# P1 and P2 of the second product on two levels in blocks k=1 and k=2 of an fp32 AdaLN and expert FFN kernel

## Chip, core and metric

The kernel runs on one core of a Trainium2 chip, in fp32. The metric is the device time of one execution in microseconds (us). Five engines work side by side, each through its own queue in order: TensorE (PE; its weight loads are listed as PEld), VectorE (DVE), ScalarE (ACT), GpSimd (POOL) and SyncE (SP), which issues the transfers. They wait for each other by semaphores.

## What is computed

The reference, cut to what matters (B, N, D = 64, 64, 512; six experts of rank 16, the two largest gates are kept):

```python
def cond(v, q, W3, b3, W2, b2):
    q_emb = relu(q @ W3 + b3)
    v_sum = sum(v, axis=1, keepdims=True)
    x = (n * v + v_sum) * q_emb[:, None, :]
    return relu(x @ W2 + b2)

def ffn(x, W_base, b_base, A_s, B_s, A_r, B_r, W_router, b_router):
    base_out = x @ W_base + b_base
    shared_out = (x @ A_s) @ B_s
    gates = softmax(x @ W_router + b_router)
    # w_per_e: the gates of the two largest experts, 0 for the others
    hw = einsum('bsd,edr->bser', x, A_r) * w_per_e[..., None]
    routed_out = einsum('bser,erf->bsf', hw, B_r)
    return base_out + shared_out + routed_out

out = x + ffn(cond(x, cond_1024, ...), ...)
```

There are two wide products of 4096 rows by 512 by 512: the first with `W2` (it makes `y`), the second with `W_base`. The narrow product multiplies `y` by 118 columns: shared and expert factors, and the router's logits.

## The kernel before

The 4096 rows are four blocks of 1024, k = 0 to 3 ("blocks 1 to 4" in the change's title words, so blocks 2 and 3 are k=1 and k=2). Features lie on the 128 partitions, rows along the free axis. Each wide product is done by Strassen's scheme in Winograd's form: its operands are quartered and seven products P1 to P7 of half size take the place of eight. `row_sums` (L261) forms the sums of the row side, `weight_sums` (L133) those of the weights. A product of half size is, for each of two output chunks j, `product` (L174): two matmuls of 128x512. An fp32 matmul appears in the trace as two records.

The scheme can be applied again inside a product ("two levels"): a half-size product then becomes seven inner products of 128x256, which the code calls `q(n, t)`: n = 1 to 7 is the inner product, t the outer product in the order in which they run. The text calls them Q1 to Q7. They share two PSUM banks per outer product, a and b, each of two halves of 256 columns. Q1 and Q2 go to a's low half, Q5 and Q3 to its high half, Q6 to b's low half (on top of a copy of Q1, `seed_y`), Q7 and Q4 to b's high half (on top of a copy of Q1+Q6, `seed_z`). What has to be read in between leaves by `take_w5` (Q5), `take_u` (Q1+Q6), `take_22` (after Q7), `take_1` (after Q2 and Q3) and `take_21` (after Q4). Where the outer product has something to be added to (`plus`), a take is a DVE addition; where it has nothing (`plus` is None), ACT copies the part.

The first product is on two levels in k = 1, 2, 3 (`first_inner`, L431). The second product is on one level in k = 0, 1, 2 (`second`, L658), and partly on two in k = 3 (`second_inner`, L759), where Q1, Q5, Q6 of P1 stand among the narrow products (`two[6]`, `two[7]` in the loop at L1058).

In `second` PSUM banks are called x (P1, then P2 on top), y (a copy of P1, then P6), z (a copy of y, then P7 and P4) and w (P5, then P3), each for j = 0 and 1. ACT makes the copies (`seed`, L670). `with_x` (L676) adds the input rows, which have been loaded to `res` (L648), by DVE. `gate` (L607) makes softmax and top 2 on DVE with one Exp on ACT, `weigh` (L584) multiplies on DVE, `turn` (L593) transposes on TensorE into `hwT`, `difference` (L602) makes `hwd` on POOL, and `routed` (L682) adds the expert part to the banks.

The next block's preparation is spread over all this by hand: `prepare` (L284) fills a list `behind`, and `fill` (L279) takes items from it at fixed places; `share` (L698) does so in `second`. An item is a pair of batches (ACT, L218: one batch of 64 rows of one chunk is multiplied by q and N and gets its sum added, in place in `x`), or a pair of reductions with their multiplication (DVE, L213 and L214), or a row sum. `nq` (L212) is N times q. The order of the instructions on each engine is that of the code.

Six PSUM banks ("pp") rotate among the banks of the products; SBUF tiles with one tag share one place.

Of the kernel before, what the change touches and what calls it, by code (L numbers as in the profile page):

```python
# [1 line left out]

# [7 lines left out]
F32 = mybir.dt.float32  # L10
# [5 lines left out]
P = 128  # L16
# [21 lines left out]
def adaln_ffn(ctx: ExitStack, tc: tile.TileContext, xa, x0, x1, head, w3, w2, wb, a, bcat, bb, br, outT):  # L38
# [108 lines left out]
    def inner_weight_sums(w, t, it, pairs=(5, 6, 7, 4), engine=nc.vector):  # L147


        order = (*pairs, 1, 2, 3)  # L150
        at = {i: n for n, i in enumerate(order)}
        step = 3 // (len(pairs) - 1)

        def side(o, n):
            b = {1: t[o][:, 0, :P], 2: t[o][:, 1, :P], 3: t[o][:, 1, P:]}
            return b[n] if n in b else it[:, {5: 0, 6: 1, 7: 2, 4: 3}[n], at[o]]

        low = w.rearrange("p (o k) m -> p o k m", k=KH)
        n = len(pairs)
        groups = ((slice(0, n), lambda c, m: t["sums"][:, ::step, c, ts(m, P)]),  # L160
                  (slice(n, n + 2), lambda c, m: low[:, :, c, ts(m, P)]),
                  (slice(n + 2, n + 3), lambda c, m: t[3][:, c, ts(m, P)].unsqueeze(1)))
        steps = []
        for o, b in groups:
            i = [it[:, n, o] for n in range(4)]
            steps += [
                lambda i=i, b=b: engine.tensor_tensor(i[0], b(0, 1), b(0, 0), ALU.subtract),
                lambda i=i, b=b: engine.tensor_tensor(i[1], b(1, 1), i[0], ALU.subtract),
                lambda i=i, b=b: engine.tensor_tensor(i[2], b(1, 1), b(0, 1), ALU.subtract),
                lambda i=i, b=b: engine.tensor_tensor(i[3], b(1, 0), i[1], ALU.subtract),  # L170
            ]
        return side, steps
# [26 lines left out]
    def modulate(k):  # L199
# [6 lines left out]
        def sums(c, half):  # L206

            bs = ts(half, BB // 2)
            xc = v[:, c].rearrange("p h (b n) -> p b h n", n=NH)[:, bs]
            q = q_sb[:, c, ts(k, BB)]  # L210
            if half == 0:
                nc.vector.tensor_scalar(nq[:, c], q, float(N), None, ALU.mult)  # L212
            nc.vector.tensor_reduce(vsum[:, c, bs], xc, AX.XY, ALU.add)  # L213
            nc.vector.tensor_tensor(vsum[:, c, bs], vsum[:, c, bs], q[:, bs], ALU.mult)  # L214
# [69 lines left out]
    def prepare(k, also=()):  # L284
# [6 lines left out]
        ss[k], row_steps = row_sums(vs[k], "s")  # L291
        early, late = row_steps(slice(0, 1)), row_steps(slice(1, 2))
# [56 lines left out]
    def first_mixed(y):  # L349
# [30 lines left out]
        p1 = mid.tile([P, KH, cols], F32, tag="p1", name="p1_0")  # L380
# [277 lines left out]
    def second(k, y, ph, res):  # L658
# [44 lines left out]
        gate(k, ph)  # L703
        prod(1, 0, "x")
        seed("y", "x", 0)
        prod(1, 1, "x")
        seed("y", "x", 1)
        prod(6, 0, "y", start=False)
        seed("z", "y", 0)
        prod(2, 0, "x", start=False)  # L710
        weigh(k, ph)
        u12, u22 = {}, {}
        u12[0] = with_x("y", 0, KH, 0)
        share()
        prod(7, 0, "z", start=False)
        u22[0] = with_x("z", 0, KH, 1)
        prod(6, 1, "y", start=False)
        seed("z", "y", 1)
        u12[1] = with_x("y", 1, KH + 1, 0)
        share()  # L720
        prod(2, 1, "x", start=False)
        prod(7, 1, "z", start=False)
        u22[1] = with_x("z", 1, KH + 1, 1)
        hwT = turn(k)
# [33 lines left out]

    def second_inner(k, y, res):  # L759
# [3 lines left out]
        t_side = wide["t"]  # L763
# [5 lines left out]
        x11, x12, x21, x22 = res[0, 0], res[1, 0], res[0, 1], res[1, 1]  # L769
        plus = {1: None, 2: x11, 5: None, 4: x21, 3: x12}  # L770
        out = {1: p1, 2: x11, 5: p5, 4: x21, 3: x12}

        place = {1: (0, (0, 1, 2, 3)), 2: (1, (0, 1, 2, 3)), 5: (1, (3, 1, 2, 0)), 4: (2, (0, 1, 2, 3)),
                 3: (3, (0, 1, 2, 3))}
        sy = {}
        add = lambda o, a, b, engine=nc.vector: engine.tensor_tensor(o, a, b, ALU.add)

        def sums_of(o, a, engine=nc.vector):
            i, at = place[o]
            return inner_row_steps(lambda n: plain[:, at[n], i], a, engine)  # L780
# [7 lines left out]

        def s_side(o, n):
            a = sy[o]  # L790
            direct = {1: a[:, 0, lo], 2: a[:, 1, lo], 4: a[:, 1, hi]}
            if n in direct:
                return direct[n]
            i, at = place[o]
            return plain[:, at[{5: 0, 6: 1, 7: 2, 3: 3}[n]], i]
# [17 lines left out]
        bank, hws = {}, {}  # L813

        def open_banks(t):
            for n in "ab":
                bank[n, t] = ps_p.tile([P, TB], F32, tag="pp", name=f"j{n}_{k}_{t}")

        def accumulate(p, w, s, start=False):
            nc.tensor.matmul(p, w, s, start=start, stop=True, skip_group_check=True)  # L820

        def q(n, t):
            o = order[t]
            b, cols = {1: ("a", lo), 2: ("a", lo), 5: ("a", hi), 3: ("a", hi), 6: ("b", lo), 7: ("b", hi), 4: ("b", hi)}[n]
            accumulate(bank[b, t][:, cols], t_side(o, n), s_side(o, n), n == 1)

# [16 lines left out]

        def seed_y(t):
            nc.scalar.copy(bank["b", t][:, lo], bank["a", t][:, lo])

        def seed_z(t):
            nc.scalar.copy(bank["b", t][:, hi], bank["b", t][:, lo])

        def take(t, src, at, j, cols):  # L850

            c, e = out[order[t]][:, j, cols], plus[order[t]]
            if e is None:
                nc.scalar.copy(c, src[:, at])
            else:
                add(c, src[:, at], e[:, j, cols])

        def passed_on(t, j, cols):
            o = order[t]
            if o == 5:  # L860
                add(x12[:, j, cols], x12[:, j, cols], p5[:, j, cols])
                add(x22[:, j, cols], x22[:, j, cols], p5[:, j, cols], nc.gpsimd)
            if o in (5, 4, 3):
                f, h, t = {5: (KH, 1, x22), 4: (0, 1, x21), 3: (KH, 0, x12)}[o]
                j = slice(j, j + 1) if isinstance(j, int) else j
                queue = nc.scalar if o == 3 and cols == hi else nc.sync
                queue.dma_start(
                    outT[k, f + j.start : f + j.stop, h, :, cols].rearrange("f p t -> p f t"), t[:, j, cols]
                )

        take_w5 = lambda t: take(t, bank["a", t], hi, 1, hi)
        take_u = lambda t: take(t, bank["b", t], lo, 1, lo)

        def take_22(t):
            r = out[order[t]][:, 1, hi]
            add(r, bank["b", t][:, hi], r)
            passed_on(t, 1, hi)

        def take_1(t):
            a, c, e = bank["a", t], out[order[t]], plus[order[t]]  # L880
            if e is c:
                add(c[:, :, lo], a.rearrange("p (j t) -> p j t", j=KH), c[:, :, lo])
            else:
                take(t, a, lo, 0, lo)
                add(c[:, 1, lo], a[:, hi], c[:, 1, lo])
            passed_on(t, slice(0, KH), lo)

        def take_21(t):
            take(t, bank["b", t], hi, 0, hi)
            passed_on(t, 0, hi)  # L890
# [21 lines left out]
        def main_part(ph):  # L912
# [5 lines left out]
            def first():  # L918
                q(7, 0)
                q(3, 0)  # L920
                q(6, 1)
                seed_z(1)
                q(2, 0)
                take(0, bank["a", 0], lo, 0, lo)
                take_w5(1)
                take_22(0)

            gate(k, ph, (first, lambda: add(p1[:, 1, lo], bank["a", 0][:, hi], p1[:, 1, lo])))
# [90 lines left out]
    inner_t, inner_steps = inner_weight_sums(  # L1019
        w2_sb, t2, const.tile([P, 4, 7, P], F32, tag="inner_t", name="inner_t")  # L1020
    )


    wide = {}
# [3 lines left out]
        0: [lambda: nc.gpsimd.tensor_tensor(bcat_d, bcat_pairs[:, :, 0], bcat_pairs[:, :, 1], ALU.subtract)]  # L1028
    }

    def wide_sums():
        place = xpool.tile([P, NC, 2, TB], F32, tag="x", name="inner_tb").rearrange("p c h t -> p (c h t)")
        wide["t"], steps = inner_weight_sums(
            wb_sb, tb, place[:, : 20 * P].rearrange("p (n o m) -> p n o m", n=4, o=5), (5, 4), nc.gpsimd
        )
        beside[1], beside[2] = steps[:4], steps[4:]

    for k in range(NB):
# [18 lines left out]
        two = second_inner(k, y, res) if k == NB - 1 else None  # L1057
        for n, (h, s) in enumerate(groups):  # L1058
            if rest and n == 2:
                rest()  # L1060
                if two:
                    two["sums"]()
            if two and n in two:
                two[n]()
# [5 lines left out]
        if two:  # L1070
# [5 lines left out]
        fill(4 if k else 9)  # L1076
        second(k, y, ph, res)
# [51 lines left out]
```

## Time and profile before

| | |
|---|---|
| median of 3 runs | 259.87 us (259.43 to 259.95) |
| profiled execution | 259.86 us, its span 258.1 us |
| mean granted TensorE clock | 0.997 |
| narrow product to the end of the second product, k=1 | 94.44 to 134.59 us of the span: 40.15 |
| the same, k=2 | 155.98 to 196.13: 40.15 |
| TensorE busy in each of these two stretches | 39.99 of 40.15 |
| HBM traffic | 110 GB/s over the span |

A line of the timeline has the start and length in us, engine, line of the code, operation, output and inputs with shapes, how many instructions were merged, and in brackets the engine's idle time before it with what ended it. The length of a merged PE line is not its spacing, since ends overlap: spacing is read from the starts of the following lines. A line of the page's first part has the busy time, share of the span and number of instructions of each engine. The chain line is the span split by what the last instruction was waiting for, step by step backwards.

### The profile page before, as it was taken

Reading aid. Unit: us, or ns where it says so; the run is one execution under the profiler, and the core shown is the slowest. Engines: PE = TensorE matmul, PEld = TensorE weight load, DVE = VectorE, ACT = ScalarE, POOL = GpSimd, SP = SyncE. Lnnn points to the kernel's source line nnn. Section 1 sums busy time; section 2 is a strip of 40 time slices with the busy share of each in tenths; the row PEclk is TensorE's granted clock in tenths of the full one; section 3 lists DMA queues with packets and bytes.
Section 4 is the critical chain, followed back from the end, with each engine's and each line's share of the span. In section 5 each row is a group of like instructions: output and inputs, shape, how many; then the busy total and the mean of one; then the engine's idle time right before and its main releaser. Section 6 shows DMA issues by size and latency. Waiting matters only on the chain.

```text
span 258.1 us, 3326 instructions
## 1 busy us (share of the span) xinstructions
PE 252.6 (98%) x1034; PEld 170.6 (66%) x1034; DVE 199.6 (77%) x404; ACT 142.7 (55%) x391; POOL 68.8 (27%) x88
## 2 busy tenths in 40 slices
PE   7999999999999999999999999999999999999994
PEld 3755896454468889445448888744446889975783
DVE  2899898789958976967995894996896476887473
ACT  2399587597037897279106889439603527443220
POOL 1000000012008520005104650000920864039950
PEclk9999999999999999999999999999999999999998
DMA  6998729403320035000431023300232003600054
GB/s 174 369 341 297 290 79 379 192 3 122 122 81 0 4 143 183 0 3 0 163 123 41 0 83 118 130 0 3 104 140 81 0 6 128 193 1 3 0 183 142
DMA packets 14675, 28.54 MB, mean 111 GB/s; under 512 B 1489, under 2 KB 3537, under 8 KB 14658
## 3 DMA queue, kind: packets, MB, share of 16 engines
q1 hardware_dynamic: 14370, 28.08, 30.9%
q10 hardware_dynamic: 288, 0.26, 0.3%
q8 instruction: 8, 0.13, 0.2%
q14 instruction: 9, 0.07, 0.1%
HBM read 19.94 MB, written 8.39 MB: 110 GB/s over the span
## 4 chain that ended last, share of the span: by engine, by line
PE 94%; ACT 2%; DMA 2%; SPq 0%; issue 0%; DVE 0%
PE ia L453 13%; PE ph L1066 11%; PE ib L453 10%; PE oz L176 9%; PE ox L176 8%; PE ow L176 8%; PE py L361 5%; PE oy L176 5%; PE ja L820 4%; PE ow L683 4%; PE jb L820 4%; PE ox L683 2%; PE oz L683 2%; DMA w_sb<-in_w_dram 2%; PE yw L176 1%; PE pt L597 1%
## 5 line engine op out<-in xcount | busy, mean ns | idle before, releaser
L218 ACT ACTIVATE x<-x,vsum,nq 128x64 f32<-128x64 f32 x192 | 67.5, 431 | 6.8 <-DVE vsum L214 6.8
L604 POOL TENSOR_TENSOR hwd<-hwT 113x512 f32<-113x512 f32 x4 | 5.6, 1393 | 109.4 <-ACT hwT L599 109.4
L1066 PEld LDWEIGHTS ph<-a_sb,y 128*128 128x128 f32 x256 | 30.3, 192 | 1.3 <-ACT y L347 0.7
L1066 PE MATMUL ph<-a_sb,y 128*128 128x118 f32 x256 | 30.8, 276 | 0.3 <-ACT y L347 0.3
L459 ACT COPY ib<-ia 128x256 f32<-128x256 f32 x21 | 7.6, 361 | 42.3 <-PE ia L453 42.3
L444 DVE TENSOR_TENSOR u<-ib,u 128x256 f32<-128x256 f32 x42 | 16.4, 418 | 18.6 <-PE ib L453 18.5
L176 PE MATMUL ox<-y,wb_sb 128*128 128x512 f32 x48 | 22.1, 593 | 0.0
L444 DVE TENSOR_TENSOR u<-ia,u 128x256 f32<-128x256 f32 (+1 forms) x36 | 16.1, 461 | 2.9 <-ACT u L491 1.6
L347 ACT ACTIVATE y<-u,head_sb 128x256 f32<-128x256 f32 (+1 forms) x30 | 15.8, 584 | 3.8 <-DVE u L419 3.1
L453 PE MATMUL ib<-inner_s,inner_t 128*128 128x256 f32 x60 | 17.8, 384 | 0.0
L213 DVE TENSOR_REDUCE vsum<-x 128x8 f32<-128x512 f32 x24 | 16.2, 675 | 0.0
L176 PEld LDWEIGHTS ox<-y,wb_sb 128*128 128x128 f32 x48 | 8.9, 190 | 10.0 <-issue 9.6
L176 PE MATMUL oz<-sy,tb 128*128 128x512 f32 x32 | 15.2, 599 | 0.0
L361 PE MATMUL py<-v,w_sb 128*128 128x512 f32 (+1 forms) x40 | 14.4, 510 | 0.8 <-DMA w_sb<-in_w_dram 0.8
L176 PE MATMUL oy<-sy,tb 128*128 128x512 f32 x32 | 14.9, 594 | 0.0
L307 POOL TENSOR_TENSOR inner_two<-x 128x256 f32<-128x256 f32 x3 | 2.2, 727 | 45.0 <-PE ib L453 45.0
L462 ACT COPY ib<-ib 128x256 f32<-128x256 f32 x21 | 7.6, 363 | 9.9 <-PE ib L453 9.9
L453 PEld LDWEIGHTS ib<-inner_s,inner_t 128*128 128x128 f32 x60 | 11.2, 190 | 2.2 <-ACT ib L462 0.8
L256 ACT ACTIVATE v<-x,vsum,nq 128x64 f32<-128x64 f32 x32 | 11.0, 430 | 1.9 <-DVE vsum L254 1.9
L361 PEld LDWEIGHTS py<-v,w_sb 128*128 128x128 f32 x40 | 7.4, 190 | 6.5 <-issue 4.5
L176 PE MATMUL oz<-y,tb 128*128 128x512 f32 x24 | 11.3, 592 | 0.0
L176 PE MATMUL ow<-sy,tb 128*128 128x512 f32 x24 | 11.3, 592 | 0.0
(236 smaller groups left out, 545.0 us busy)
## 6 DMA issues: line engine op xcount, KB each, us to landing
xu<-in_x_dram SPq DMA_DIRECT2D x16, 512.0 KB, 3.7
out_dram<-xu SPq DMA_DIRECT2D x29, 256.0 KB, 2.0
x<-in_x_dram SPq DMA_DIRECT2D x12, 512.0 KB, 7.6
x<-in_x_dram SPq DMA_DIRECT2D x7, 256.0 KB, 5.6
w_sb<-in_w_dram SPq DMA_DIRECT2D x4, 256.0 KB, 5.6
wb_sb<-in_wb_dram SPq DMA_DIRECT2D x4, 256.0 KB, 4.8
out_dram<-xu SPq DMA_DIRECT2D x4, 128.0 KB, 1.7
w_sb<-in_w_dram SPq DMA_DIRECT2D x1, 384.0 KB, 5.2
```

Source lines behind the costliest of these rows:

```text
L176: nc.tensor.matmul(ps, w[i][:, c, ts(j, P)], s[i][:, c, :], start=start and c == 0, stop=c == KH - 1, skip_group_check=True,)
L213: nc.vector.tensor_reduce(vsum[:, c, bs], xc, AX.XY, ALU.add)
L218: nc.scalar.activation(x, x, AF.Identity, bias=vsum[:, c, b : b + 1], scale=nq[:, c, b : b + 1])
L256: nc.scalar.activation(v[:, c, :, ts(b, NH)], batches_of(c, b, b + 1)[:, :, 0], AF.Identity, bias=vsum[:, c, b : b + 1], scale=nq[:, c, b ...
L347: nc.scalar.activation(y[:, f, h, cols], src, AF.Relu, bias=b2_sb[:, f : f + 1])
L361: nc.tensor.matmul(p[:, :, lo * NH : hi * NH], w2_sb[:, c, ts(f, P)], v[:, c, :, lo * NH : hi * NH], start=(c == 0 and lo == 0), stop=(c = ...
L444: add = lambda o, a, b: nc.vector.tensor_tensor(o, a, b, ALU.add)
L453: nc.tensor.matmul(bank[b, t][:, cols], t_side(o, n), s_side(o, n), start=n == 1, stop=True, skip_group_check=True,)
L459: nc.scalar.copy(bank["b", t][:, lo], bank["a", t][:, lo])
L683: nc.tensor.matmul(ps[name, j], bcat_sb[:, ts(f, P)], hw, start=False, stop=True, skip_group_check=True)
L820: nc.tensor.matmul(p, w, s, start=start, stop=True, skip_group_check=True)
L1066: nc.tensor.matmul(ph[:, h * NS + s, :HC], y[:, c, h, ts(s, P)], a_sb[:, c, :], start=(c == 0), stop=(c == NC - 1),)
```

## The change

P1 and P2 of the second product go on two levels in k=1 and k=2. The helpers of `second_inner` move to `inner_tools`, so that both use them, and the row side's places to `row_places`; the new `two_products` holds P1 and P2. P1's Q1, Q5 and Q6 stand among the last two narrow products. `second` gets a second branch for these blocks: banks y and x no longer accumulate P1 and P2 from products on one level, but get P1 by an ACT copy from SBUF; P2 is added to the loaded rows by POOL. The transposes come between the two products of P7. `fill(4)` moves from behind the row sums to the place ahead of P1's Q1.

P1 and P2 lie in a tile with the tag `s`, which the next block's row sums also use; so `prepare` now takes that tile at the first row sum, no longer at its own start. The weight sums of P1 and P2 (`low_t`) are formed once, by POOL in k=0, and k=3 uses them too. `p1_0` of k=0 moves to another tag. N times q is formed for all chunks in one instruction.

```diff
@@ modulate
-            if half == 0:
-                nc.vector.tensor_scalar(nq[:, c], q, float(N), None, ALU.mult)
+            if half == 0 and c == CHUNKS[0]:
+                nc.vector.tensor_scalar(nq, q_sb[:, :, ts(k, BB)], float(N), None, ALU.mult)
@@ prepare
-        ss[k], row_steps = row_sums(vs[k], "s")
-        early, late = row_steps(slice(0, 1)), row_steps(slice(1, 2))
+        made = []
+
+        def row_step(c, n):
+            if not made:
+                ss[k], row_steps = row_sums(vs[k], "s")
+                made.extend(row_steps(slice(c, c + 1)) for c in range(KH))
+            made[c][n]()
+
+        early, late = ([lambda c=c, n=n: row_step(c, n) for n in range(4)] for c in range(KH))
...
+    def two_products(k, y, res):
+
+        parts = mid.tile([P, 4, KH, TB], F32, tag="s", name=f"parts_{k}")
+        plain = mid.tile([P, 4, 4, R2], F32, tag="inner_s", name=f"inner_y_{k}")
+        p1, p2 = parts[:, 0], parts[:, 1]
+        operand = {1: y[:, :KH, 0], 2: y[:, KH:, 0]}
+        s_side, sums_of = row_places(plain, lambda o: operand[o], {o: (o - 1, (0, 1, 2, 3)) for o in (1, 2)})
+        tools = inner_tools(k, "h", (1, 2), low_side, s_side, {1: None, 2: None}, {1: p1, 2: p2})
+        for o in (1, 2):
+            for step in sums_of(o, lambda c, r, o=o: operand[o][:, c, ts(r, R2)], nc.gpsimd):
+                step()
+
+        def first_part():
+            tools.open_banks(0)
+            tools.q(1, 0)
+            tools.q(5, 0)
+            tools.seed_y(0)
+            tools.take_w5(0)
+
+        def second_part():
+            tools.q(6, 0)
+            tools.seed_z(0)
+            tools.take_u(0)
+
+        def third_part(ph):
+
+            tools.open_banks(1)
+            tools.q(1, 1)
+            tools.q(5, 1)
+            tools.seed_y(1)
+
+            def first():
+                tools.q(7, 0)
+                tools.q(3, 0)
+                tools.q(6, 1)
+                tools.seed_z(1)
+                tools.q(2, 0)
+                tools.take_11(0)
+                tools.take_w5(1)
+                tools.take_u(1)
+                tools.take_22(0)
+
+            gate(k, ph, (first, lambda: tools.take_12(0)))
+            tools.q(4, 0)
+            tools.take_21(0)
+            tools.q(7, 1)
+            tools.take_22(1)
+            tools.q(3, 1)
+            tools.q(2, 1)
+
+        def fourth_part():
+            tools.q(4, 1)
+            tools.take_21(1)
+            tools.add(res[0, 0], res[0, 0], p2, nc.gpsimd)
+
+        return {6: first_part, 7: second_part, "gate": third_part, "end": fourth_part, "p1": p1,
+                "one": lambda: tools.take_1(1)}
+
@@ second
+        if two:
+            copy_in = lambda name, j, source: nc.scalar.copy(bank(name, j), source)
+            two["gate"](ph)
+            weigh(k, ph)
+            two["one"]()
+            for j in range(KH):
+                copy_in("y", j, two["p1"][:, j])
+                prod(6, j, "y", start=False)
+            two["end"]()
+            for j in range(KH):
+                seed("z", "y", j)
+                u12[j] = with_x("y", j, KH + j, 0)
+                share()
+            prod(7, 0, "z", start=False)
+            u22[0] = with_x("z", 0, KH, 1)
+            hwT = turn(k)
+            prod(7, 1, "z", start=False)
+            u22[1] = with_x("z", 1, KH + 1, 1)
+            for j in range(KH):
+                copy_in("x", j, two["p1"][:, j])
+        else:
...
@@ inner_tools
+        def take(t, src, at, j, cols):
+            c, e = out[order[t]][:, j, cols], plus[order[t]]
+            if e is None:
+                nc.scalar.copy(c, src[:, at])
+            else:
+                add(c, src[:, at], e[:, j, cols])
...
+        def take_1(t):
+            c = out[order[t]]
+            if plus[order[t]] is c:
+                add(c[:, :, lo], bank["a", t].rearrange("p (j t) -> p j t", j=KH), c[:, :, lo])
+            else:
+                take_11(t)
+                take_12(t)
+            passed_on(t, slice(0, KH), lo)
@@ the loop over blocks
             if two and n in two:
+                if n == 6:
+                    fill(4)
                 two[n]()
...
-        fill(4 if k else 9)
-        second(k, y, ph, res)
+        if not two:
+            fill(9)
+        second(k, y, ph, res, two)
```

`take_11` is the `take` of a's low half (Q1+Q2), `take_12` a DVE addition of a's high half (Q5+Q3) to what `take_u` left.

## The prediction

> **What bounds it now.** I read the page first: busy time, then the chain that ended last.
>
> ```profile
> PE 252.6 (98%) x1034; PEld 170.6 (66%) x1034; DVE 199.6 (77%) x404; ACT 142.7 (55%) x391; POOL 68.8 (27%) x88
> PE 94%; ACT 2%; DMA 2%; SPq 0%; issue 0%; DVE 0%
> ```
>
> TensorE is on 94% of the chain. Nothing is late for it, so a removed matmul is worth its own spacing, and every wait that is put in front of a matmul is paid in full. A busy PE hides small gaps, so I then read the timeline by start times, in the changed stage. Block k=1 lasts there from 94.44 (first narrow matmul) to 134.59 (first product of k=2); k=2 repeats it (155.98 to 196.12).
>
> ```profile
> 107.96 0.57 ACT L671 COPY oz<-oy 128x512 f32<-128x512 f32 x1 [1.15 <-PE oy L176]
> 109.03 0.68 DVE L679 TENSOR_TENSOR xu<-oy,xu 128x512 f32<-128x512 f32 x1
> ...
> 111.41 2.76 ACT L218 ACTIVATE x<-x,vsum,nq 128x64 f32<-128x64 f32 x8 [2.88 <-DVE vsum L214]
> 112.91 1.88 PE L176 MATMUL ox<-y,wb_sb 128*128 128x512 f32 x4
> ...
> 114.08 0.57 ACT L671 COPY oz<-oy 128x512 f32<-128x512 f32 x1
> 114.59 3.42 ACT L218 ACTIVATE x<-x,vsum,nq 128x64 f32<-128x64 f32 x10
> 114.70 1.99 PE L176 MATMUL oz<-sy,tb 128*128 128x512 f32 x4
> ```
>
> To be seen: the seed of bank z1 stands on ACT behind eight batches of the next block's modulation, and these behind a DVE addition and two reductions. Seed z0 to the end of seed z1 takes 107.96 to 114.65 here, and TensorE has other work for just that long: its product starts at 114.70 instead of 112.91+1.72 = 114.63, and its first record takes 0.11 more (1.99 against 1.88). This wait costs 0.18. The change rearranges this chain.
>
> **Matmuls removed and added, per block.** Two records make one fp32 matmul. A 512-column product (four records) is spaced 1.72, an inner 256-column one (two records) 0.43 (134.59, 135.02 in a row below). Removed: P1 and P2, four products, 6.88. Added: 14 inner ones, 6.03. Gain 0.85; with the old wait gone, 1.03.
>
> **Work beside.** Per block POOL gets eight 128x256 sums (0.73 each by the L307 to L310 rows at 216.85) and the addition of P2, 128x1024 (2.36, the L776 POOL row): 8.2. It is idle from 92 to 119 there. The first four sums start at 94.1, the others with y's lower rows at 97.5, end 100.8; their matmuls come at 101.2 and 104.3. `hwd` and the later weight sums behind them on POOL are due only near 125. DVE: four 0.42 additions more; the `nq` merge removes three instructions spaced 0.08. Block k=0: four low-weight sums on POOL, 3.4 (the L167 to L170 rows), free until 77.46. SP issues the same transfers in the same order. All of this at 0; should POOL slow DVE (a 0.45 addition took 0.87 under it at 230.40), up to 0.4 in the gate, which has 6 us until its transposes.
>
> ACT gets 12 copies of 256 columns (0.37, spaced 0.27) and two more of 512. The page has ACT at 55%; but it runs in order, so where each copy stands is what counts.
>
> **The new waits (k=1, clock of this trace).** Block k=3 already has this scheme; its rows give the steps:
>
> ```profile
> 229.62 1.11 ACT L910 COPY oy<-parts 128x512 f32<-128x512 f32 x2
> 229.88 0.59 PE L820 MATMUL ja<-y,wb_sb 128*128 128x256 f32 x2
> 230.31 3.65 PE L176 MATMUL oy<-sy,tb 128*128 128x512 f32 x8
> 232.29 0.57 ACT L910 COPY oz<-oy 128x512 f32<-128x512 f32 x1 [1.56 <-PE oy L176]
> 233.80 0.59 PE L820 MATMUL jb<-y,inner_tb 128*128 128x256 f32 x2
> 234.24 1.88 PE L176 MATMUL oz<-sy,tb 128*128 128x512 f32 x4
> ```
>
> No gap there: bank y's copy starts before P2's last inner product, and z's before its Q4, because P2 leaves by DVE additions onto x (`plus` is x11). In the changed blocks `plus` is None for P2 too: its parts leave by ACT copies, and these stand ahead of the copies TensorE waits for. Constants: ACT starts 0.63 after a 256-column pair's first record (135.02 to 135.65 below), TensorE 0.05 after ACT's end (114.65 to 114.70), and 0.11 is lost at a restart.
>
> Narrow products with Q1, Q5, Q6 of P1 end at 102.60+1.29 = 103.88. Before Q6, `fill(4)` stands on ACT ahead of seed y: eight batches end at 101.82, Q5's result is there at 101.86, so 0. Then Q1, Q5 of P2, Q7, Q3, Q6, Q2, Q4 reach 106.88, where P2's Q7 is due.
>
> - W1. ACT does seed z when Q6 is out (106.22), the P1 part when Q2 is out (106.65), W5 (106.92), U (107.19 to 107.56). In the built program Q7 waits for U's copy, which reads the other half of the same bank. A row of the trace shows such waiting by banks:
>
> ```profile
> 134.59 0.59 PE L453 MATMUL ia<-x,w_sb 128*128 128x256 f32 x2
> 135.02 0.59 PE L453 MATMUL ia<-inner_s,inner_t 128*128 128x256 f32 x2
> 135.65 0.36 ACT L459 COPY ib<-ia 128x256 f32<-128x256 f32 x1 [12.04 <-PE ia L453]
> ```
>
> The copy needs only the first matmul's half (out at 135.22), ACT was idle, and it started after the second. So Q7 starts at 107.61, cost 0.73+0.11 = **0.84**. The Trainium skill says why one orders it so (PSUM — Partial Sum Buffer, "PSUM bank collisions raise a hardware error": two engines on one bank and quadrant collide even at different addresses, so a dependency is put between them). By columns alone W1 would be 0.
> - W2. Q3 108.15, Q2 108.58. P2's copy (`take_11`) waits for Q2 (109.21), the copy into y0 stands behind it (109.48 to 110.06). Product 6 is due at 109.01, starts at 110.11: 1.10+0.11 = **1.21**. Behind it y1's copy is in time.
> - W3. Products 6 end at 113.66, Q4 of P2 at 114.09. Its copy `take_21` (114.29) is ahead of seed z0 (114.56 to 115.12); product 7,0 starts at 115.17: 1.08+0.11 = **1.19**.
> - W4. Seed z0 (start 114.56) heads the chain shown above: DVE's addition waits for its end (115.17), two reductions queue behind that, first batch at 115.17+2.38-0.08 = 117.47 (109.03 to 111.41, one `nq` less), z1's seed 2.67 later, ends 120.71. TensorE has only product 7,0 (1.83) and the transposes (0.87), to 117.87. Product 7,1 starts at 120.76: 2.89+0.11 = **3.00**.
> - W5. DVE now does y1's addition and a reduction before z0's addition, ending 2.1 after z1's seed; product 4,0 is due 1.83 after it: 0.3+0.11 = **0.4**.
>
> The x banks' copies stand behind ten batches and two `hwT` copies on ACT, ending at 125.97; the first due at 126.44. The early row sums of the next block now wait for these copies (tile `s` is shared with P1, P2) and start at 126.0 instead of 117.33, 3.1 later relative to TensorE's end; the late ones wait for ACT's last batch, 0.9 later. The first inner sum (131.46 against 135.88) has 4.4 of room. At 0; below it nothing is gained.
>
> Sum per block: 6.64 - 1.03 = +5.6; two blocks +11.2. The profiled execution took 259.86 (span 258.1), practically the median 259.87: 259.86+11.2 = **271.1**.
>
> **A rule against the change.** The trace has no TensorE pause near 3 us; its granted clock is 1.00 in both blocks. TensorE: Matmul & The Clock Gate ("Why this matters for your kernels") warns of pauses above about 3 us, after which the clock is halved; W4 is 2.9. By the row the sum stays; by the rule, if a window of about 3.4 us runs at half speed per block (an estimate from that page), 1.7 us more each: 274.5. The page asks for a whole idle window (3.4), so I take 0 and keep 3.4 for the range.
>
> **Rivals.**
> 1. *Faster.* TensorE pays only for columns, as the rows of k=3 suggest. That needs ACT to have y0's copy done when P2's Q2 is issued, and z1's seed within 3.1 us of Q4's start. Then 2 x 1.03 off: 257.8. Against it: Q4's chain is 0.63+0.27+0.57+0.05+2.30+2.67+0.57+0.05 = 7.1, over 3.1; it decides from there. 4%, with no change 1%.
> 2. *Only the first waits.* W1 to W3 happen, but batches run early enough that W4 and W5 vanish: 3.24-1.03 = +2.2 per block, 264.3. Against it: the reductions stand behind the addition that waits for z0. 7%.
> 3. *The clock falls as well:* 274.5. 8%.
>
> The forecast itself has 80%, from 267.8 (no W1, no W5: -2.5, and 0.4 less latency per block) to 272.7 (0.8 more per block); with rival 3, the range is **267.5 to 275.0**. Faster by over 0.2% (0.5 us, about what a measurement tells) 0.04, within 0.01, slower 0.95.
>
> **What will show it.** In the windows of k=1 and k=2: about 45.8 us each instead of 40.15, TensorE busy about 5 less than the window. Gaps of about 0.7, 1.1, 1.1 and 2.9 before P2's Q7, product 6,0, product 7,0 and product 7,1, each ended by ACT. Blocks k=0 and k=3 unchanged. Wrong if product 6 follows P2's Q2 without a gap, if the batches start before z0's seed, or if PEclk drops below 9.

## The result, and the profile after

| | before | after |
|---|---|---|
| median | 259.75 us (259.43 to 259.95) | 274.81 us (274.42 to 275.96) |
| profiled execution, its span | 259.86, 258.1 | 274.86, 273.1 |
| k=1, narrow product to the end of the second product | 40.15 | 47.63 |
| the same, k=2 | 40.15 | 47.62 |
| mean granted clock | 0.997 | 0.986 |

The ratio is 1.0585 (1.0559 to 1.0612). The two changed stretches grew by 7.48 and 7.47 us, 14.95 of the 15.0 us; k=0 and k=3 are as before. First the page of the kernel after: busy time, the granted clock in 40 slices, and the chain.

```profile
PE 256.8 (94%) x1058; PEld 176.7 (65%) x1058; DVE 203.7 (75%) x403; ACT 152.5 (56%) x419; POOL 87.2 (32%) x106
PEclk9999999999999999997999999999799999999999
PE 80%; DVE 9%; ACT 6%; DMA 2%; issue 1%; SPq 1%; DVEq 0%
```

PE's share of the chain fell from 94% to 80%, and DVE and ACT now hold 15%: TensorE waits for them. There is a second sign: two slices of the clock show 7. PE's busy time even rose by 4.2 us although the change removed matmul columns, so some of the work ran slower. The timeline of TensorE in k=1 shows both (start, length, idle time before in brackets):

```profile
107.79 0.67 PE L863 MATMUL hb<-inner_y,low_t 128*128 128x256 f32 x2 [0.67 <-ACT parts L879]
...
110.27 3.70 PE L181 MATMUL oy<-sy,tb 128*128 128x512 f32 x8 [0.95 <-ACT oy L776]
...
115.36 1.98 PE L181 MATMUL oz<-sy,tb 128*128 128x512 f32 x4 [0.95 <-ACT oz L742]
117.18 1.04 PE L610 MATMUL pt<-ident,hw 128*113 128x128 f32 x8
121.38 2.92 PE L181 MATMUL oz<-sy,tb 128*128 128x512 f32 x4 [3.17 <-ACT oz L742]
124.10 2.68 PE L181 MATMUL oz<-y,tb 128*128 128x512 f32 x4
126.62 1.88 PE L181 MATMUL ow<-sy,tb 128*128 128x512 f32 x4
```

The four waits stand where the prediction put them, each ended by ACT. Behind the longest, two products are spaced 2.72 and 2.52 (from the starts) instead of 1.72. The windows view (us of each engine's busy time, then the clock) says why:

```profile
core 0: us, PE busy (x) PEld busy (x) DVE busy (x) ACT busy (x) POOL busy (x), PEclk, DMA share, GB/s
118.90:122.30 3.40, 0.92 (x2) 0.49 (x3) 0.94 (x2) 3.40 (x11) 0.00 (x0) 1.00 0.00 0
122.30:125.70 3.40, 3.40 (x5) 1.28 (x4) 1.81 (x4) 3.40 (x11) 0.00 (x0) 0.50 0.00 0
125.70:129.10 3.40, 3.40 (x9) 1.52 (x8) 2.32 (x3) 3.40 (x10) 3.31 (x3) 1.00 0.00 0
```

The clock is halved for 3.4 us, from 122.3 on, when TensorE had been working again for 0.9 us. In k=2 the same happens from 190.55 to 193.97. Last, the chain behind seed z1, on DVE and on POOL:

```profile
115.34 0.69 DVE L750 TENSOR_TENSOR xu<-oy,xu 128x512 f32<-128x512 f32 x1 [4.17 <-ACT oz L742]
115.94 0.68 DVE L218 TENSOR_REDUCE vsum<-x 128x8 f32<-128x512 f32 x1
116.66 0.61 DVE L219 TENSOR_TENSOR vsum<-vsum,q_sb 128x8 f32<-128x8 f32 x1
117.19 0.67 DVE L218 TENSOR_REDUCE vsum<-x 128x8 f32<-128x512 f32 x1
```

```profile
114.89 2.35 POOL L856 TENSOR_TENSOR xu<-xu,parts 128x1024 f32<-128x1024 f32 x1 [13.86 <-ACT parts L879]
```

The third DVE line has 8 columns and took 0.61 instead of 0.17. It ends at 117.27, just when POOL's addition of P2 does (117.24); the reductions beside it keep their length. The trace of the kernel before already holds such a case, beside a sum on POOL:

```profile
141.18 0.74 DVE L214 TENSOR_TENSOR vsum<-vsum,q_sb 128x8 f32<-128x8 f32 x1
141.17 0.73 POOL L310 TENSOR_TENSOR inner_two<-x,inner_two 128x256 f32<-128x256 f32 x1
```

### The profile page after: what moved, and what is told of

It reads as the page before. It is cut to its first block, busy times and chain, and to the rows that moved or that the text cites. A ratio compares the mean times of both kernels' runs of the same rounds, so it can differ in the third digit from the quotient of the medians.

```text
span 273.1 us, 3429 instructions
## 1 busy us (share of the span) xinstructions
PE 256.8 (94%) x1058; PEld 176.7 (65%) x1058; DVE 203.7 (75%) x403; ACT 152.5 (56%) x419; POOL 87.2 (32%) x106
## 4 chain that ended last, share of the span: by engine, by line
PE 80%; DVE 9%; ACT 6%; DMA 2%; issue 1%; SPq 1%; DVEq 0%
PE ia L466 13%; PE ph L1191 10%; PE ib L466 10%; PE oz L181 9%; PE ow L181 8%; PE oy L181 5%; PE ja L863 4%; PE ow L754 4%; PE jb L863 3%; PE ha L863 3%; PE ox L181 3%; ACT x L223 3%; DMA x<-in_x_dram 2%; PE ox L754 2%; PE oz L754 2%; PE hb L863 2%
## 5 line engine op out<-in xcount | busy, mean ns | idle before, releaser
L1191 PEld LDWEIGHTS ph<-a_sb,y 128*128 128x128 f32 x256 | 30.9, 192 | 1.6 <-ACT y L359 0.7
L1191 PE MATMUL ph<-a_sb,y 128*128 128x118 f32 x256 | 31.4, 276 | 0.3 <-ACT y L359 0.3
L181 PE MATMUL oz<-sy,tb 128*128 128x512 f32 x32 | 18.1, 694 | 8.2 <-ACT oz L742 8.2
L856 POOL TENSOR_TENSOR xu<-xu,parts 128x1024 f32<-128x1024 f32 (+2 forms) x6 | 10.5, 1768 | 30.1 <-ACT parts L879 28.8
L181 PEld LDWEIGHTS oz<-sy,tb 128*128 128x128 f32 x32 | 6.2, 206 | 14.9 <-ACT oz L742 9.4
L750 DVE TENSOR_TENSOR xu<-oy,xu 128x512 f32<-128x512 f32 x6 | 4.2, 692 | 15.2 <-ACT oz L742 15.2
L181 PE MATMUL oz<-y,tb 128*128 128x512 f32 x24 | 12.1, 629 | 0.0
L181 PEld LDWEIGHTS oy<-sy,tb 128*128 128x128 f32 x32 | 5.8, 190 | 9.1 <-issue 6.2
```

Of the source, the lines that this page charges most:

```text
L181: nc.tensor.matmul(ps, w[i][:, c, ts(j, P)], s[i][:, c, :], start=start and c == 0, stop=c == KH - 1, skip_group_check=True,)
L1191: nc.tensor.matmul(ph[:, h * NS + s, :HC], y[:, c, h, ts(s, P)], a_sb[:, c, :], start=(c == 0), stop=(c == NC - 1),)
```

## Experiments

The theory after the result: W1 to W4 as forecast, plus a fall of the clock that W4 causes, plus a DVE instruction held by POOL. Rivals: the inner products themselves are slow; the waits only move elsewhere when removed; the clock has nothing to do with the pause.

**e1: the batches behind both seeds.** The first share moves behind z1's seed, the second behind the copies into x.

```diff
             for j in range(KH):
                 seed("z", "y", j)
                 u12[j] = with_x("y", j, KH + j, 0)
-                share()
+            share()
...
             for j in range(KH):
                 copy_in("x", j, two["p1"][:, j])
+            share()
```

> The changed kernel, with one edit in k=1 and k=2: both seeds of z come before the first share of batches, and the second share comes after the copies into the x banks. Theory (the eight batches between the two seeds make the long pause before product 7,1, and the pause makes the clock fall): the pause of 3.3 and the 1.7 of half clock go in each block, 274.8 - 10.0 = 264.8; the pauses before P2's Q7, product 6,0 and product 7,0 stay at 1.27, 1.55 and 1.55 between starts less the spacing (0.84, 1.1, 1.1), and PEclk stays at 1.00. Rival (ACT has too much to do in this stretch, wherever the batches stand): the pause moves to the first routed product of bank x, 268 or more.

Measured 266.3 us (ratio 1.0247, 1.02 to 1.0294). W4 and the clock fall are gone, and W1 to W3 stay: k=1 takes 42.50, 2.35 more than before, which is W1+W2+W3 less the gain. The rest is not in these stretches, but in the next block's first product, where TensorE waits for DVE:

```profile
142.70 0.70 PE L466 MATMUL ib<-x,inner_t 128*128 128x256 f32 x2 [0.41 <-DVE u L457]
...
146.02 0.70 PE L466 MATMUL ib<-s,inner_t 128*128 128x256 f32 x2 [0.46 <-DVE u L457]
```

The batches were put off, so the next block's row sums came late on DVE (the second half starts 6.0 before the end of the stretch instead of 9.4), and DVE is late with its additions there: that product takes 22.70 instead of 21.39 in k=2, and 21.68 instead of 21.00 in k=3. With 2 x 2.35 and these 2.0 the 259.7 become 266.4; the forecast of 264.8 had no term for it.

**e2: the pause filled, everything else in place.** Ten bf16 matmuls on constants run in z1's bank while its seed is awaited; their result is overwritten.

```diff
-            for j in range(KH):
-                seed("z", "y", j)
-                u12[j] = with_x("y", j, KH + j, 0)
-                share()
+            seed("z", "y", 0)
+            u12[0] = with_x("y", 0, KH, 0)
+            share()
             prod(7, 0, "z", start=False)
+            keep = bank("z", 1)
+            for _ in range(10):
+                nc.tensor.matmul(keep, ones[:, :P], ones, start=True, stop=True, skip_group_check=True)
+            nc.scalar.copy(keep, ps["y", 1])
+            u12[1] = with_x("y", 1, KH + 1, 0)
+            share()
             u22[0] = with_x("z", 0, KH, 1)
```

The loop over the seeds is only written out; the order on ACT and DVE is that of the changed kernel.

> The changed kernel with ten bf16 matmuls of 128x512 on constants, added in the long pause of k=1 and k=2, in the bank of z1 before its seed is copied there (they compute nothing that is used). All waits stay. Theory (the half clock after the pause is a cost of its own, caused by the pause): the matmuls take 2.2 of 3.2, PEclk stays at 1.00, 1.7 go in each block: 274.8 - 3.4 = 271.4. Rival (the wait alone is the loss): no change, 274.8, or more by what the matmuls add.

Measured 272.16 us (1.0473, 1.0424 to 1.0521), 2.65 less than after. Product 7,1 starts as late as before, but runs at full clock:

```profile
119.06 1.03 PE L610 MATMUL pt<-ident,hw 128*113 128x128 f32 x8
121.09 1.98 PE L181 MATMUL oz<-sy,tb 128*128 128x512 f32 x4 [0.99 <-ACT oz L791]
123.21 1.98 PE L181 MATMUL oz<-y,tb 128*128 128x512 f32 x4
```

So the pause causes the fall. The gain is less than two falls (3.4) because W5 comes back: product 4,0 starts 2.12 after 7,1, 0.3 over the 1.72 and 0.1 of a restart. In the changed kernel the slowed product 7,1 hid it.

**e3: the copies TensorE waits for are put first.** The copies into y directly behind P1's Q4, U's copy of P2 behind Q7, seed z0 ahead of P2's Q4; batches as in the changed kernel.

```diff
-                tools.take_u(1)
...
             tools.take_21(0)
+            for j in range(KH):
+                copy_in(j, p1[:, j])
             tools.q(7, 1)
+            tools.take_u(1)
             tools.take_22(1)
...
-                copy_in("y", j, two["p1"][:, j])
                 prod(6, j, "y", start=False)
+            seed("z", "y", 0)
             two["end"]()
             for j in range(KH):
-                seed("z", "y", j)
+                if j:
+                    seed("z", "y", j)
```

> The changed kernel, with the ACT copies put elsewhere in k=1 and k=2: y's two copies directly behind P1's Q4, P2's U behind P2's Q7, seed z0 ahead of P2's Q4; batches stay between the seeds of z. Theory: the three short pauses go (0.84, 1.21, 1.19), the chain of seed z0, addition, reductions, batches, seed z1 starts earlier and leaves a pause of about 2.2 before product 7,1, at full clock: 257.8 + 2 x 2.3 = 262.4. Rival (the clock falls after pauses of this length too): 3.4 more, 265.8. Rival (ACT's load counts, not its order): over 268.

Measured 267.69 and 270.43 us, ratio 1.0353 (1.0291 to 1.0416). No gap is left at Q7, product 6,0 and product 7,0, so W1 to W3 were the order on ACT. But the forecast was missed by 5 to 8 us, since W4 grew. The timelines of TensorE, DVE and POOL, k=1 and (second line) k=2:

```profile
118.48 3.43 PE L181 MATMUL oz<-sy,tb 128*128 128x512 f32 x4 [3.58 <-ACT oz L744]
...
184.54 1.98 PE L181 MATMUL oz<-sy,tb 128*128 128x512 f32 x4 [3.59 <-ACT oz L744]
```

```profile
113.02 2.13 DVE L219 TENSOR_TENSOR vsum<-vsum,q_sb 128x8 f32<-128x8 f32 x1
```

```profile
112.80 2.34 POOL L859 TENSOR_TENSOR xu<-xu,parts 128x1024 f32<-128x1024 f32 x1 [11.93 <-ACT parts L882]
```

The little DVE instruction now started 0.2 after POOL's addition and took 2.13, to within 0.01 of its end. In the changed kernel it met only the tail of that addition. The second surprise: the two pauses are of equal length, and only the first is followed by half clock.

**e4: both orders together.** e3 with e1's places of the shares.

> Both edits of the two runs before together: copies earlier, and batches behind the seeds of z and behind the copies into x. Theory (the removed matmuls are worth 0.85 per block and all of the loss was the order on ACT): no pause in the second product of k=1 and k=2, 257.8. Rival (14 more copies and 24 later batches per block come back elsewhere, in the row sums of the next block or in its first product): 259 to 262.

Measured 262.64 us (1.0099, 1.0069 to 1.0129); of W1 to W4 nothing is left.

```profile
118.11 1.98 PE L181 MATMUL oz<-y,tb 128*128 128x512 f32 x4 [0.80 <-DVE xu L752]
...
141.44 0.70 PE L466 MATMUL ib<-x,inner_t 128*128 128x256 f32 x2 [0.42 <-DVE u L457]
144.76 0.70 PE L466 MATMUL ib<-s,inner_t 128*128 128x256 f32 x2 [0.46 <-DVE u L457]
```

The theory (257.8) is missed by 4.8, and the rival's 259 to 262 by 0.6. Z0's addition stands behind three reductions on DVE now (W5 in another size, 1.06 per block by starts), the late batches cost the same 2.0 as in e1, and 0.2 per block is left at Q3; that is 4.5 of the 4.8.

**e5: P2's addition off POOL.** e3, with the addition on DVE behind product 7,0.

```diff
-            tools.add(res[0, 0], res[0, 0], p2, nc.gpsimd)
...
             prod(7, 0, "z", start=False)
+            nc.vector.tensor_tensor(res[0, 0], res[0, 0], two["p2"], ALU.add)
             u22[0] = with_x("z", 0, KH, 1)
```

> The kernel of e3 with P2's addition to the loaded rows taken from POOL and given to DVE, behind product 7,0. In e3 a DVE instruction of 128x8 (L219) took 2.13 us instead of 0.17 and ended with POOL's 128x1024 addition. Theory (DVE waits there for POOL's instruction to end): the reductions end 1.96 earlier per block, so product 7,1 starts with a gap of about 1.7 instead of 3.7 and the clock stays at 1.00: 267.7 less 2 x 1.96 less one clock fall of 1.7 = 262.1 us. Rival (the reductions' chain itself is as long, POOL is no cause): within 0.5 of e3's runs, 267.7 to 270.4. Below 260 neither holds.

Measured 264.78 us (1.0182, 1.0142 to 1.0222). All `vsum` multiplications are at 0.17, and the batches start at 113.03 instead of 115.19:

```profile
116.32 1.98 PE L181 MATMUL oz<-sy,tb 128*128 128x512 f32 x4 [1.61 <-ACT oz L743]
119.58 1.98 PE L181 MATMUL oz<-y,tb 128*128 128x512 f32 x4 [1.27 <-DVE xu L751]
```

The first gap is as forecast and the clock is at 1.00 in both stretches, so POOL's addition was the cause. The second line is where the forecast was missed by 2.7: product 4,0 starts 3.26 behind 7,1 in both blocks, because the moved addition (1.22) stands in front of z0's on DVE. With the restart that costs 1.54 per block, of which e3 had 0.40 already in k=2; 2.68 are new. The experiment made that wait itself.

**e7 and e8: shorter pauses.** The changed kernel with a first share of three items (six batches), or two (four batches), instead of four.

```diff
-        most = {9: 4, 8: 5, 7: 6}
+        most = {9: 3 if two else 4, 8: 5, 7: 6}
```

> The changed kernel with 6 batches instead of 8 ahead of the seed of z1 in both blocks. The pause ahead of product 7,1 should be 3.17 - 0.67 = 2.5 us. Theory A (the clock falls where a window of about 3.4 us of a clock of its own has less than some third of work; 27% fell, 45% did not): it falls in some blocks and executions and not in others; 270.7 us without, 1.4 more for each fall, up to 273.5. Theory B (only a pause above about 3 us makes it fall): never, 270.7 in all executions. Theory C (any pause above 1 us does): always, 273.5.

> The changed kernel with 4 batches instead of 8 ahead of the seed of z1 in both blocks: pause of about 3.17 - 1.35 = 1.8 us. Theories A and B: the clock stays at 1.00 in all executions, 274.8 - 2 x (1.35 + 1.69 - 0.3) = 269.3 us. Theory C: it falls, 272.1.

The idle times before product 7,1 are 2.51 and 1.85, as expected. e7 (ratio 1.0493, 1.0437 to 1.055) took 272.28, 272.42, 273.16 and 273.85 us; the first two with mean clocks of 0.997 and 1.00, the others with 0.986 and 0.987. The profile of the 273.16 has two falls. So the clock falls in some executions only, and theory A holds against B and C. e8 (271.21 us, ratio 1.0429, 1.0387 to 1.0471) had 0.998 in three executions and 0.993 in one; in the profiled one no fall is seen. By an estimate from the length of a fall, 0.993 is one fall (half of 3.41 in 269 us is 0.6%). One execution of the kernel before (261.73 us) shows 0.993 as well, so a single fall seems to come also where no such pause was made; no trace here shows why. The times without a fall lie above the forecasts, in e7 by 1.6 and in e8 by 1.9. In e8 most of it is W5: product 4,0 starts 2.92 behind 7,1 instead of the 2.12 of e2, because two reductions of the second share, not one, now stand ahead of z0's addition.

Where it falls and where not is seen in windows that are laid on the edges of the half clock. First e3, the window before the fall and the fall in k=1, then two windows on the same grid, 19 and 20 periods after the first, round the pause in k=2:

```profile
114.60:118.02 3.42, 0.30 (x3) 0.10 (x1) 1.32 (x3) 2.83 (x9) 0.54 (x1) 1.00 0.00 0
118.02:121.43 3.41, 2.95 (x4) 1.40 (x5) 2.05 (x4) 3.41 (x11) 0.00 (x0) 0.50 0.00 0
179.45:182.87 3.42, 1.50 (x10) 1.01 (x8) 2.52 (x3) 1.62 (x5) 1.74 (x1) 1.00 0.00 0
182.87:186.28 3.41, 1.74 (x4) 0.68 (x4) 1.73 (x4) 3.41 (x11) 0.00 (x0) 1.00 0.00 0
```

Then e7, k=1:

```profile
116.99:120.40 3.41, 1.00 (x9) 0.80 (x7) 0.81 (x3) 2.53 (x8) 0.03 (x1) 1.00 0.00 0
120.40:123.81 3.41, 3.31 (x4) 1.46 (x5) 2.81 (x6) 3.41 (x12) 0.00 (x0) 0.50 0.00 0
```

Every half-clock stretch found behind a pause lasts 3.41. The two in one execution begin 68.26 apart in the changed kernel and 68.27 in e7, which is 20 times 3.41, although the pauses are 69.03 and 68.31 apart: they keep to a grid, not to the pause. A window with 0.30 (9%), 0.92 (27%) or 1.00 us (29%) of work was followed by half clock; windows with 1.50 (44%) and 1.74 (51%) were not. The same pause of 3.6 can lie in one window or across two.

The end of several profiled executions, where TensorE has run out of work, narrows this down. The clock falls there too, behind 1.15 us (34%) in e2, 1.30 (38%) in e8 and 1.34 (39%) in e5, and in the kernel before behind the same 44% that had no fall in e3:

```profile
253.21:256.62 3.41, 1.49 (x7) 0.95 (x6) 1.12 (x2) 0.00 (x0) 0.00 (x0) 1.00 0.45 151
256.62:258.08 1.46, 0.00 (x0) 0.00 (x0) 0.00 (x0) 0.00 (x0) 0.00 (x0) 0.50 0.03 10
```

So the limit lies near 44% of work, as far as busy time with modelled ends can tell.

**e10: W1 alone.** One line of the changed kernel is moved.

```diff
                 tools.take_w5(1)
-                tools.take_u(1)
...
             tools.q(7, 1)
+            tools.take_u(1)
```

> The changed kernel with one line moved: U's copy of P2 stands behind Q7 in the program instead of ahead of it, so that Q7 has no copy of its own bank to wait for. Theory (W1 is that wait and nothing else): Q7 follows at 0.43 and everything behind it comes 0.9 earlier per block; W2 to W4 and the clock stay: 274.8 - 1.8 = 273.0 us. Rival (Q7 waits for something else as well, ACT's queue above all): W1 stays, 274.8. Rival (W2 takes it back, since U's copy is now between Q2 and the copy into y0): 274.3 to 274.8. Each fall of the clock more or less than in the changed kernel shifts this by up to 1.7.

Measured 273.1 us (1.0527, 1.0494 to 1.056), 1.7 less than after, with two falls of the clock in the profile as there. P2's Q7 now follows 0.43 behind P1's Q4:

```profile
106.26 0.60 PE L863 MATMUL hb<-y,low_t 128*128 128x256 f32 x2
106.69 0.59 PE L863 MATMUL hb<-inner_y,low_t 128*128 128x256 f32 x2
```

W2, W3 and the pause have the same idle times (0.95, 0.95, 3.17). So W1 was the copy that stood ahead of Q7 in the program, and nothing else.

**e9: N times q alone,** on the kernel before.

```diff
-            if half == 0:
-                nc.vector.tensor_scalar(nq[:, c], q, float(N), None, ALU.mult)
+            if half == 0 and c == CHUNKS[0]:
+                nc.vector.tensor_scalar(nq, q_sb[:, :, ts(k, BB)], float(N), None, ALU.mult)
```

> The kernel before with the change's other part alone: N times q of all chunks in one instruction (three DVE instructions, spaced 0.08, less per block). Theory (DVE has cover there): no difference, 259.7 us within 0.2%. Rival (the merged instruction stands in front of the first reduction and delays the batches): up to 0.3 more per block, 260.6.

Measured 259.68 beside 259.73 us, ratio 1.0002 (0.9989 to 1.0015). This part of the change makes no difference that these runs can tell.

**e6: the change with all of this put right.** From e5: two reductions are moved to where DVE sat idle ahead of y's row sums; the batches stand in ACT's gaps between the copies; z0's addition goes before P2's.

```diff
-        for places, steps in (((4, 4 if k == 1 else 5), sums[c1]), ((16, 16), sums[c2]), ((19, 20), sums[c3]),
+        for places, steps in (((4, 4 if k == 1 else 5), sums[c1]), ((16, 16) if k == 1 else (12, 13), sums[c2]), ((19, 20), sums[c3]),
...
+            fill(1)
             weigh(k, ph)
...
             seed("z", "y", 0)
+            fill(3)
             two["end"]()
+            seed("z", "y", 1)
             for j in range(KH):
-                if j:
-                    seed("z", "y", j)
                 u12[j] = with_x("y", j, KH + j, 0)
-                share()
+            places.pop(0)
+            share()
             prod(7, 0, "z", start=False)
-            nc.vector.tensor_tensor(res[0, 0], res[0, 0], two["p2"], ALU.add)
             u22[0] = with_x("z", 0, KH, 1)
+            nc.vector.tensor_tensor(res[0, 0], res[0, 0], two["p2"], ALU.add)
```

> The kernel of e5 with the order round the seeds changed: the two reductions of the third chunk are ahead of the row sums of y in the changed blocks, one item of batches stands behind the gate, three between the seeds of z0 and z1, five behind z1; P2's addition on DVE behind z0's addition. Theory (the rest of e4's loss is z0's addition waiting behind reductions, 0.9 per block, and the next block's row sums coming 4 us late, 1.3 and 0.7): no pause of TensorE above 0.2 in either stretch and 1.03 less per block than before: 257.8 us. Rival (DVE itself is too full, so something is late again in the next block's inner products): 260 to 262.5.

Measured 258.06 us, beside 259.69 before: ratio 0.9939 (0.9922 to 0.9955), a little faster than the kernel before. The page, then TensorE's timeline at Q3:

```profile
PE 250.8 (98%) x1058; PEld 175.2 (68%) x1058; DVE 204.6 (80%) x405; ACT 152.3 (59%) x419; POOL 81.5 (32%) x104
```

```profile
106.71 0.59 PE L868 MATMUL hb<-inner_y,low_t 128*128 128x256 f32 x2
107.27 0.67 PE L868 MATMUL ha<-inner_y,wb_sb 128*128 128x256 f32 x2
107.78 0.59 PE L868 MATMUL ha<-y,wb_sb 128*128 128x256 f32 x2
108.21 3.60 PE L181 MATMUL oy<-sy,tb 128*128 128x512 f32 x8
```

The stretches take 39.35 and 39.34 instead of 40.15, 0.8 less each; of the 1.03 of the forecast, 0.2 stays at Q3, where the starts are 0.56 and 0.51 apart instead of 0.43. Two blocks make 1.6, and that is the difference of the medians. ACT does as much as in the changed kernel and DVE a little more: the loss was order, and P2's addition on POOL. What each of the three moves of e6 brings was not measured apart.

## Why the prediction was right, and where not

The forecast was 271.1, and the range up to 275.0 held the result; 3.7 us are to be explained. The range held it only because it took in the third rival: the forecast's own part ended at 272.7. That this rival's 274.5 came within 0.3 is partly luck, since W4 was 0.43 per block too small and W5 0.4 too large. Of the signs of being wrong that the prediction named, one came: PEclk fell below 9. All terms of k=1 by starts, the slower first record included:

| term | predicted | measured |
|---|---|---|
| matmuls and the old wait | -1.03 | -0.98 |
| W1 | 0.84 | 0.91 |
| W2 | 1.21 | 1.22 |
| W3 | 1.19 | 1.22 |
| W4 | 3.00 | 3.43 |
| W5 | 0.4 | 0 |
| clock | 0 | 1.70 |
| sum | 5.6 | 7.5 |

- **W1, W2, W3** were right in place, cause and size. e10 shows W1 by itself; e3 shows that the three go together when the copies are reordered, but W2 and W3 weren't taken apart from each other.
- **W4** had the right chain. Its miss of 0.43 is one DVE instruction that POOL's addition of P2 held (0.61 instead of 0.17). The prediction had put that addition beside idle time, and had looked for contention only in the gate. The trace of the kernel before had such a case (0.74 at 141.18), which was overlooked. In e3 the same cost 1.96, and e5 took it away. The Trainium skill has it (GPSIMD Engine Reference, "8. Key points": POOL shares its SBUF interfaces with VectorE, which contends in instructions with two SBUF inputs). The trace agrees in which ones: `vsum` has two inputs in SBUF; the reduction with one, and additions that read PSUM, keep their length. In all these lines the wait lasts to the end of POOL's instruction. That the interface is the reason is the page's word; e5 shows only that the addition on POOL is the cause.
- **The clock at 0** is the step that failed. The prediction weighed the page on the clock gate and took it to ask for a whole idle window, and so gave this case, its third rival, 8%. Here a window with 27% of work was enough. e2 shows that the pause causes the fall. That it depends on how the pause lies in the windows is read from e3, where one of two equal pauses had it, and from the executions of e7. The price was right: 1.7 per block was estimated, 1.70 measured. Filling the pause won back 1.3 of it in e2, since W5 returned.
- **W5** was 0 only because the fall of the clock gave DVE time; in e2 it is there as forecast, 0.4 with the restart.
- **The first rival, faster,** needed another order of copies and batches. e6 is that kernel: its 257.8 came out as 258.06. The second rival fails: the reductions did stand behind z0's addition.
- **Work beside at 0** held for the transfers, the `nq` merge (e9) and the next block's row sums: k=2's first product takes 21.40, as before. It held with little reserve: in e1 and e4 the batches ended later, and it cost 1.3 in k=2 and 0.7 in k=3.

## What to carry to other kernels

When products are cut smaller, count for each copy that TensorE awaits what stands ahead of it in its engine's queue, bookkeeping copies and bulk work alike; here nearly the same instructions in another order, with one addition moved from POOL to DVE, made 274.8 into 258.1 us. If a pause of TensorE can leave a clock window with less than about 44% of work, give it the price of a halved window (1.7 us here), and not only if it is longer than the window. Before a long addition is put on GpSimd, look for the small two-input instructions of DVE that start meanwhile, and for who waits for them.

## What was not expected of the hardware

- The half clock came in pieces of 3.41 us on a fixed grid, and began up to 0.9 us after TensorE had resumed; up to 39% of work in a window did not prevent it, 51% did, and at 44% both were seen.
- A DVE multiplication of 8 columns took 2.13 us instead of 0.17 while POOL added 128x1024; the reductions beside it kept 0.68.
- POOL is held too. In the changed kernel longer additions of both engines, with both inputs in SBUF, end by turns: at 128.12, 128.67, 129.25 and 129.80 in the lines below. Alone, such a sum takes 0.73 on POOL and 0.68 or 0.69 on DVE.

```profile
126.94 1.18 POOL L151 TENSOR_TENSOR inner_tb<-tb 128x256 f32<-128x256 f32 x1
127.57 1.10 DVE L275 TENSOR_TENSOR s<-s,x 128x512 f32<-128x512 f32 x1
128.19 1.06 POOL L152 TENSOR_TENSOR inner_tb<-tb,inner_tb 128x256 f32<-128x256 f32 x1
128.59 1.21 DVE L276 TENSOR_TENSOR s<-x 128x512 f32<-128x512 f32 x1
```
